# Transposed features made a stage ahead, two added steps, and small roots as powers on GpSimd

## The chip, the cores and the metric

The kernel runs on one core of a Trainium2 chip. A core has five engines that work through queues of their own, each strictly in its order: PE (TensorE, matrix products and transposes, with weight loads shown as PEld), DVE (VectorE, elementwise work and reductions), ACT (ScalarE, activation functions and copies), POOL (GpSimd) and SP (SyncE, which issues the DMAs here). Engines wait for one another through semaphores. The metric is the device time of one execution, in microseconds; the number shown for a kernel is the median of its runs.

## What is computed

The input is 64 independent graphs, each with 256 nodes of 128 features `x` and a 0/1 adjacency matrix `adj` (about 12% ones, symmetric, full diagonal). Four layers run one after the other; each adds its result to `x` and normalizes each node's features (mean 0, variance 1):

```python
# layer 0: for each node the maximum over its neighbours
pre = p[:, :, None, :] + q[:, None, :, :] + b        # p = x(W1-W2), q = x W2
h   = max(relu(pre) * adj[..., None], axis=2)
# layer 1: three ELU projections, two aggregations over adj, one product, tanh
# layer 2: ELU twice, then twice  D^-1/2 (adj+I) D^-1/2 (h W) + b,  D the degrees
# layer 3: for each pair of nodes a normalized message
pre = m_j[:, None, :, :] + m_i[:, :, None, :] + b1
msg = gelu(layernorm(pre, g1, be1))
agg = einsum('bijo,bij->bio', msg, adjacency)
out = layernorm(concat([x, agg]) @ W2 + b2, g2, be2)
```

Every normalization needs one over the square root of a variance, and layer 2 one over the square root of each node's degree.

## The kernel before

The features lie on the partitions or the nodes do, 128 at a time, so a graph has two halves (H = 2). The adjacency is sparse: a node's neighbours are numbered and nodes are sorted by their number of neighbours, so that one graph's pairs fit 4800 columns for each half (WIDTH), cut into five tiles of 1024 columns (the fifth has 704). `hot` is a one-hot matrix (fp8) that picks for each column its neighbour.

The work on one graph is split into four stages, written as generators: `first` (load `x` and `adj`, sort, build `hot`), `second` (`layer_0`, then `layer_1`), `third` (`layer_2`, then the first four tiles of layer 3) and `last` (the other six tiles, the messages, the output). In a steady step, `last` of graph g, `third` of g+1, `second` of g+2 and `first` of g+3 are interleaved by `together`: each generator runs up to its next `yield`, and the one that is relatively least far, by the number of its yields in `STAGES`, goes next. A scheduler of the framework then fixes each engine's order from that; it is the same in every steady graph. Where this text speaks of the built order, it means the order in which a built program holds the instructions of each engine.

The places that matter here (line numbers of the kernel before):

- `inverse_root` (L70 to L73): a square root on ACT (L72) and a reciprocal on DVE (L73). `layernorm` calls it on `rs`, 128x2, five times a graph (the variance is made ready at L172, the scale is used at L178, or at L182 and L183 for the output); `layer_2` on the degrees `dinv`, 128x2, once (L269 to L272); `sums_of` on `vr`, 128x16 or 108x16, five times, for pairs of tiles.
- [...]square root, gelu, exp and tanh need switches, which show as ACT_TABLE_LOAD on the line of the function that follows.
- `to_features` (L202 to L207): two transposes of a graph's features on PE (L205), and a copy of the result to SBUF on ACT (L207). `layer_0` begins with it for `xT_0`; the products with `w0qp` (L650) follow. Their result `q`, split into three bf16 parts (L497 to L500), is what the gathers of layer 0 (L668) read, and their maxima are folded on DVE (L492) into `lanes`.
- Layer 3's tiles: matmuls of L731 gather, DVE adds into `pre` (L735), ACT squares (L739), PE sums the squares over the features (L746), ACT makes a `row` (L748), which goes through DRAM (`line`) and comes back as `vr`, one column for each pair of nodes spread over partitions; its inverse root, times a mask (L772), goes through DRAM again (`scale_line`) and comes back broadcast as `rs_s`; DVE multiplies (L846), ACT applies the gelu (L848), DVE folds (`sums`, L492), PE multiplies with the weights (L867), ACT copies `ak` (L872), and PE brings it into the nodes' order (L877), for the output `y` (L328).

PE writes into PSUM banks of two pools, `mm` and `bigp`, four each.

Of the kernel before, what the change touches and what calls it, by code (L numbers as in the profile page):

```python
# [9 lines left out]
F32 = mybir.dt.float32  # L10
BF16 = mybir.dt.bfloat16
AF = mybir.ActivationFunctionType
ALU = mybir.AluOpType
# [6 lines left out]
P = 128  # L20
# [23 lines left out]
def kernel(  # L44
# [9 lines left out]
    nc = tc.nc  # L54
    B, N, D = x.shape
    assert N == 2 * P and D == P
    H = N // P
    Q = P // 4

    consts = ctx.enter_context(tc.tile_pool(name="consts", bufs=1))  # L60
# [6 lines left out]
    minus1 = consts.tile([P, 1], F32, name="minus1")  # L67
    nc.vector.memset(minus1, -1.0)

    def inverse_root(t):  # L70

        nc.scalar.activation(t, t, AF.Sqrt)  # L72
        nc.vector.reciprocal(t, t)  # L73

    def load(src, shape, name):
        t = consts.tile(shape, F32, name=name)
        nc.sync.dma_start(t, src)
        return t
# [4 lines left out]
    def spread(src, name):  # L83
        return load(bass.AP(tensor=src.tensor, offset=src.offset, ap=[[0, P], [1, P]]), [P, P], name)

    w0 = load(l0_w.rearrange("(c p) o -> p c o", p=P), [P, 2, P], "w0")
    w0qp = consts.tile([P, 2, P], F32, name="w0qp")
    nc.vector.tensor_copy(w0qp[:, 0], w0[:, 1])
    nc.vector.tensor_sub(w0qp[:, 1], w0[:, 0], w0[:, 1])
    b0 = column(l0_b, "b0")  # L90
    b0s = spread(l0_b, "b0s")

# [27 lines left out]
    with tc.tile_pool(name="prep", bufs=1) as prep, tc.tile_pool(  # L120
        name="ps_prep", bufs=2, space=bass.MemoryType.PSUM
    ) as ps_prep:

        def transposed(dst, src, shape, name, part=lambda t: t):
            t = prep.tile(shape, F32, name=name)
            nc.sync.dma_start(t, src)
            for d, s in part(t) if dst is None else [(dst, t)]:
                pt = ps_prep.tile([P, P], F32, name="pt")
                nc.tensor.transpose(pt, s, ident)
                nc.vector.tensor_copy(d, pt)  # L130

        transposed(w1_ioT[:, :P], l1_w_in, [P, P], "w1_in")
        transposed(w1_ioT[:, P:], l1_w_out, [P, P], "w1_out")
        transposed(w1_nodeT, l1_w_node, [P, P], "w1_node")
        transposed(
            None, l1_w_upd.rearrange("o (c k) -> o c k", k=P), [P, 3, P], "w1_upd",
            lambda t: [(w1_updT[:, c], t[:, c]) for c in range(3)],
        )
        w3 = prep.tile([P, 2, P], F32, name="w3")
        nc.sync.dma_start(w3, l3_w1.rearrange("(c p) o -> p c o", p=P))  # L140
        w3m = prep.tile([P, 2], F32, name="w3m")
        nc.vector.tensor_reduce(w3m, w3, AX.X, ALU.add)
        nc.vector.tensor_scalar(w3m, w3m, 1.0 / P, None, ALU.mult)
        for c in range(2):
            nc.vector.tensor_scalar(w3c[:, c], w3[:, c], w3m[:, c:c + 1], None, ALU.subtract)
        b3 = prep.tile([P, 1], F32, name="b3")
        nc.sync.dma_start(b3, bass.AP(tensor=l3_b1.tensor, offset=l3_b1.offset, ap=[[1, P], [1, 1]]))
        invp = prep.tile([P, P], F32, name="invp")
        nc.vector.memset(invp, 1.0 / P)
        pb = ps_prep.tile([P, P], F32, name="pt")  # L150
        nc.tensor.matmul(pb[:, :1], invp, b3, start=True, stop=True)
        nc.vector.tensor_sub(b3c, b3, pb[:, :1])


    class Shared:
# [5 lines left out]
        def psum(self):  # L161
            return self.ps_mm.tile([P, 512], F32, name="mm")
# [189 lines left out]
    def sparse(ctx):  # L352
# [36 lines left out]
        with tc.tile_pool(name="cs_prep", bufs=1) as pp:  # L389
            t = pp.tile([P, P], F32, name="upto_f")  # L390
# [4 lines left out]
            t = pp.tile([P, N], I32, name="iota_i")  # L395
# [3 lines left out]
            t = pp.tile([P, 1], I32, name="part_i")  # L399
# [25 lines left out]
            t = pp.tile([P, 1], F32, name="gbe")  # L425
# [9 lines left out]
            for i in range(3):  # L435
                t = pp.tile([3, P], BF16, name="u_part")
# [5 lines left out]
            t = pp.tile([ROWS, g_n, g_w], F32, name="tail_f")  # L442
# [12 lines left out]
        sh = Shared(work, state, ps_mm)  # L455
# [46 lines left out]
        def first(g, s):  # L502

            xn = state.tile([P, H, P], F32, name="x0", bufs=3)
# [25 lines left out]
            for hi in range(H):  # L530
                for h in range(H):
                    c = (hi * H + h) * 2
# [38 lines left out]
            permT = hold.tile([P, H, H, N], F32, name="permT")  # L571
# [17 lines left out]
            lack = hold.tile([ROWS, H, N], BF16, name="lack")  # L589
# [43 lines left out]
            for h in range(H):  # L633
# [5 lines left out]
                    saturate=False,  # L639
                )  # L640
            s["hot"] = hot

        def layer_0(s):

            xn, hot, lack, lack_t, permT = (s[n] for n in ("xn", "hot", "lack", "lack_t", "permT"))
            xT = sh.to_features(xn, "xT_0", 1)
            yield
            pq = psum()
            for h in range(H):
                nc.tensor.matmul(  # L650
                    pq[:, h * N:(h + 1) * N], xT[:, h * P:(h + 1) * P], w0qp.rearrange("p c o -> p (c o)"),
                    start=True, stop=True,
                )
            pq = pq.rearrange("p (h c o) -> p h c o", h=H, c=2)
            q3 = work.tile([P, 3, H, P], BF16, name="q3")
            split3(q3, pq[:, :, 0])
            own = work.tile([P, H, P], F32, name="own")
            for h in range(H):
                nc.vector.tensor_add(own[:, h], pq[:, h, 1], b0s)
            yield  # L660
            mk = work.tile([P, H, H, P], F32, name="mk")
            for h in range(H):
                lanes = work.tile([P, 2, N], F32, name="lanes")
                for t0 in range(0, WIDTH, 512):
                    tl = min(512, WIDTH - t0)
                    pt = ps_big.tile([P, 512], F32, name="bigp")
                    for i in range(3):
                        nc.tensor.matmul(  # L668
                            pt[:, :tl], q3[:, i, h], hot[:, h, t0:t0 + tl], start=i == 0, stop=False
                        )  # L670
                    todo = []
                    for s0, n, w, at in pieces(t0, t0 + tl):
                        if s0 >= g_s0:
                            todo.append((pt[:, at:at + n * w], low, lack_t[:, h].rearrange("p s k -> p (s k)")))
                            continue
                        for i in range(n):
                            m = SURE[s0 + i]
                            if m < w:
                                c = at + i * w
                                todo.append((pt[:, c + m:c + w], pick_of(s0 + i), lack[:, h, m:w]))  # L680
                    if not todo:
                        todo.append((pt[:, :2], pick_of(0), lack[:, h, 0:2]))
                    for i, (o_, l_, r_) in enumerate(todo):
                        nc.tensor.matmul(o_, l_, r_, start=False, stop=i == len(todo) - 1)  # L684
                    if t0 == 0:
                        nc.scalar.copy(lanes, pt.rearrange("p (s k) -> p s k", s=2))
                    else:
                        fold(lanes, pt, t0, tl, ALU.max)
                    yield
                mx = work.tile([P, N], F32, name="total_m")  # L690
                nc.vector.tensor_max(mx, lanes[:, 0], lanes[:, 1])
                pt = psum()
                for hk in range(H):
                    nc.tensor.transpose(pt[:, hk * P:(hk + 1) * P], mx[:, hk * P:(hk + 1) * P], ident)
                nc.scalar.copy(mk[:, h], by_half(pt))
                yield
            pm = psum()
            for h in range(H):
                for hi in range(H):
                    c = h * N + hi * P  # L700
                    for hk in range(H):
                        nc.tensor.matmul(
                            pm[:, c:c + P], permT[:, h, hk, hi * P:(hi + 1) * P], mk[:, h, hk],
                            start=hk == 0, stop=hk == H - 1,
                        )
            yield
            m0 = work.tile([P, H, P], F32, name="m0")
            nc.scalar.copy(m0, by_half(pm))
            nc.vector.tensor_max(m0, pm[:, N:].rearrange("p (h d) -> p h d", h=H), m0)
            nc.vector.tensor_add(m0, m0, own)  # L710
            y = work.tile([P, H, P], F32, name="y", bufs=2)
            nc.vector.scalar_tensor_tensor(y, m0, 0.0, xn, ALU.max, ALU.add)
            s["x1"] = sh.node_tile("x1")
            yield from sh.layernorm(s["x1"], y)
# [6 lines left out]
        def sums_of(s, i):  # L721
# [39 lines left out]
            n = at + tl  # L761
# [6 lines left out]
                fu[:rows],  # L768
                s["fulls"].rearrange("h w -> (h w)")[first_at:first_at + n].rearrange("(p k) -> p k", k=PIECE),
            )  # L770
            inverse_root(vr[:rows])
            nc.vector.tensor_mul(vr[:rows], vr[:rows], fu[:rows])  # L772
            out_line = dram.tile([1, GROUP * TILE], F32, name="scale_line")
            nc.sync.dma_start(out_line[:, :n].rearrange("o (p k) -> (o p) k", k=PIECE), vr[:rows])
# [108 lines left out]


        U = next(u for u in (UNROLL, 8, 4, 2, 1) if B % u == 0)
        STAGES = [(last, 34), (third, 34), (second, 42), (first, 17)]

        def steps(g0):
            ss = [{} for _ in range(U)]
# [262 lines left out]
```

## Time and profile before

| | |
|---|---|
| median of 3 runs | 5589.18 us (5588.3 to 5589.55) |
| the profiled execution | 5585.87 us, of which the span from first to last instruction is 5583.8 us |
| busy in the span | PE 4511.0, DVE 4805.5, ACT 4218.5, POOL 2.0 us |
| granted TensorE clock, mean | 0.876 of full speed |
| one graph in the steady stretch | about 85.3 us |
| ACT_TABLE_LOAD | 1152, 1283 ns each |

The page gives for each engine its busy time; groups of instructions by line have the mean time of one and what ended the idle time in front of them. "idle before" or "[4.30 <-ACT xT L207]" means that the engine stood still for 4.30 us in front of this instruction, and that the one named was the last that it waited for. In the chain that ended last, PE has 42%, DVE 34% and ACT 17% of the span.

### The profile page before, as it was taken

To read this page: it belongs to the slowest core of one execution; us is meant where nothing else is said; L and a number is where in the kernel's file an instruction comes from. 1 tells how busy PE (TensorE), PEld (TensorE's weight loads), DVE (VectorE), ACT (ScalarE), POOL (GpSimd) and SP (SyncE) were. 2 spreads that over 40 slices of the span, in tenths; PEclk is the share of its full clock that TensorE was granted. 3 is DMA by queue.
4 is the path that set the end of the run, shared out by engine and by line. 5 is a ranking of instruction groups with operands and counts; after the bars stand their busy time and mean duration, and the time that the engine had idled before them with its cause. 6 is when DMAs were issued, how large, how long until landed. Compare 5 with 4: busy or idle time off the path is not lost.

```text
span 5583.8 us, 83622 instructions
## 1 busy us (share of the span) xinstructions
PE 4511.0 (81%) x27408; PEld 2487.9 (45%) x27408; DVE 4805.5 (86%) x14654; ACT 4218.5 (76%) x6465; POOL 2.0 (0%) x10
## 2 busy tenths in 40 slices
PE   5888888888788888887887888888888878888884
PEld 3444444444444444444444444444444444444442
DVE  7788888898888888888988888889888888888886
ACT  2777777777777777777777777777777777777776
POOL 0000000000000000000000000000000000000000
PEclk8888888888888888888888888888888888888886
DMA  0212222222222122222222222221222222212212
GB/s 24 65 59 72 67 63 66 72 65 66 66 65 70 60 72 67 63 66 74 63 66 67 70 66 61 69 67 63 71 70 63 66 67 70 66 59 71 64 59 76
DMA packets 292814, 365.17 MB, mean 65 GB/s; under 512 B 151952, under 2 KB 210448, under 8 KB 292368
## 3 DMA queue, kind: packets, MB, share of 16 engines
q1 hardware_dynamic: 292368, 359.73, 20.8%
q8 instruction: 218, 3.57, 0.3%
q14 instruction: 228, 1.87, 0.1%
HBM read 345.07 MB, written 14.53 MB: 64 GB/s over the span
## 4 chain that ended last, share of the span: by engine, by line
PE 42%; DVE 34%; ACT 17%; issue 5%; DMA 3%; SPq 0%; DVEq 0%; POOL 0%; ACTq 0%; POOLq 0%
PE bigp L731 8%; PE bigp L668 8%; DVE lanes L492 8%; DVE pre L735 6%; ACT L72 6%; DVE hot L628 5%; DVE sums L492 5%; PE mm L867 4%; DVE pre L846 3%; PE mm L746 3%; PE mm L877 2%; PE mm L817 2%; PE mm L294 2%; DMA rs_s<-scale_line 2%; ACT sums L848 2%
## 5 line engine op out<-in xcount | busy, mean ns | idle before, releaser
L668 PE MATMUL bigp<-hot,q 128*128 128x512 fp8e4 (+1 forms) x3840 | 1117.5, 391 | 206.2 <-DVE lanes L492 179.7
L731 PE MATMUL bigp<-hot,c 128*128 128x512 fp8e4 (+1 forms) x3840 | 1010.6, 395 | 136.0 <-DVE pre L735 77.1
L735 DVE TENSOR_TENSOR pre<-bigp,dT 128x512 f32<-128x512 f32 (+6 forms) x1664 | 841.4, 534 | 252.2 <-PE bigp L731 245.9
L739 ACT ACTIVATE sq<-pre 128x1024 f32<-128x1024 f32 (+1 forms) x640 | 636.6, 995 | 273.2 <-DVE rs L73 196.9
L492 DVE TENSOR_TENSOR lanes<-bigp,lanes 128x512 f32<-128x512 f32 (+6 forms) x1536 | 769.3, 501 | 12.2 <-ACT vr L72 2.9
L846 DVE TENSOR_TENSOR pre<-pre,rs_s 128x1024 f32<-128x1024 f32 (+1 forms) x640 | 734.4, 1148 | 35.6 <-DMA rs_s<-scale_line 34.5
L492 DVE TENSOR_TENSOR sums<-pre,sums 128x1024 f32<-128x1024 f32 (+6 forms) x1024 | 628.3, 614 | 11.6 <-ACT pre L848 11.2
L848 ACT ACTIVATE pre<-pre,be,g 128x1024 f32<-128x1024 f32 (+1 forms) x512 | 600.0, 1172 | 11.0 <-DVE pre L846 6.9
L731 PEld LDWEIGHTS <-c 128*128 128x128 bf16 x3840 | 346.2, 102 | 544.5 <-issue 268.1
L848 ACT ACT_TABLE_LOAD x447 | 573.5, 1283 | 7.9
L72 ACT ACT_TABLE_LOAD x447 | 573.5, 1283 | 7.9
L748 ACT ACTIVATE row<-mm,eps_t 128x256 f32<-128x256 f32 (+1 forms) x640 | 293.5, 459 | 361.9 <-PE mm L746 351.0
L668 PEld LDWEIGHTS <-q 128*128 128x128 bf16 x3840 | 309.6, 100 | 514.9 <-DVE lanes L492 186.5
L746 PE MATMUL mm<-sq,ones 128*32 128x256 f32 (+1 forms) x5120 | 436.5, 418 | 113.7 <-ACT sq L739 110.7
L628 DVE TENSOR_SCALAR hot<-rank 128x512 fp8e4<-128x512 bf16 (+5 forms) x1536 | 485.4, 345 | 0.0
L684 PEld LDWEIGHTS <-pick 42*128 42x128 bf16 x2944 | 154.5, 95 | 449.6 <-issue 435.2
L650 PE MATMUL mm<-w0qp,xT 128*128 128x256 f32 x256 | 130.0, 662 | 266.3 <-ACT xT L207 266.3
L867 PE MATMUL mm<-w3u,sums 128*128 128x128 f32 x2048 | 293.8, 287 | 44.9 <-DVE sums L492 44.9
L867 PEld LDWEIGHTS mm<-w3u,sums 128*128 128x128 f32 x2048 | 258.7, 195 | 75.9 <-PE bigp L731 39.6
L684 PE MATMUL bigp<-lack,pick 42*128 42x36 bf16 (+16 forms) x2944 | 275.8, 187 | 0.0
L746 PEld LDWEIGHTS mm<-sq,ones 128*32 128x32 f32 x5120 | 107.2, 115 | 352.5 <-ACT sq L739 162.0
L73 DVE RECIPROCAL vr<-vr 128x16 f32<-128x16 f32 (+1 forms) x320 | 79.5, 249 | 161.7 <-ACT vr L72 161.6
(227 smaller groups left out, 7319.0 us busy)
## 6 DMA issues: line engine op xcount, KB each, us to landing
rs_s<-scale_line SPq DMA_DIRECT2D x512, 512.0 KB
rs_s<-scale_line SPq DMA_DIRECT2D x128, 352.0 KB
an<-in_adj SPq DMA_DIRECT2D x64, 256.0 KB
x<-in_x SPq DMA_DIRECT2D x64, 128.0 KB
line<-row SPq DMA_DIRECT2D x512, 4.0 KB
out<-o SPq DMA_DIRECT2D x64, 128.0 KB
fu<-fulls SPq DMA_DIRECT2D x192, 4.0 KB
vr<-line SPq DMA_DIRECT2D x192, 8.0 KB
```

What stands on the lines that cost most here:

```text
L72: nc.scalar.activation(t, t, AF.Sqrt)
L492: nc.vector.tensor_tensor(lanes[:, :k, :w], src[:, i:i + k], lanes[:, :k, :w], op)
L628: nc.vector.tensor_scalar(hot[:, :, at:at + w], rank[:, :, :w], s0 + i + 1.0 - FAR, None, ALU.is_equal, saturate=False)
L668: nc.tensor.matmul(pt[:, :tl], q3[:, i, h], hot[:, h, t0:t0 + tl], start=i == 0, stop=False)
L684: nc.tensor.matmul(o_, l_, r_, start=False, stop=i == len(todo) - 1)
L731: nc.tensor.matmul(pt[:, :bl], c3[:, k, h], hot[:, h, t0 + b:t0 + b + bl], start=k == 0, stop=k == 2)
L735: nc.vector.tensor_add(block(pre[:, b:], n, w, at), block(pt, n, w, at), widen(dT[:, h, :w], n))
L739: nc.scalar.activation(sq[:, :tl], pre[:, :tl], AF.Square)
L746: nc.tensor.matmul(pr[q * Q:(q + 1) * Q, :tl // 4], ones[:, :Q], v4[:, :, q], start=True, stop=True)
L846: nc.vector.tensor_mul(pre[:, :tl], pre[:, :tl], rs[:, :tl])
L848: nc.scalar.activation(msg[:, :tl], pre[:, :tl], AF.Gelu, bias=be3, scale=g3)
L867: nc.tensor.matmul(pt[:, cols], lanes[:, k, cols], w3u[:, 1], start=k == 0, stop=False)
```

## The change

- `inverse_root` becomes one operation on GpSimd: the tile to the power of a constant tile `mhalf` of -0.5. It serves the five norms and the degrees. The roots of `vr` keep ACT's square root and DVE's reciprocal, with a step boundary (`yield`) between the two.
- `xT_0` is made at the end of `first`, a stage earlier, in two buffers in place of one, and handed on in `s`; `layer_0` starts with the products.
- A step boundary is added in `layer_0` between the maximum of the two lanes and its transposes.
- The numbers of yields in `STAGES` follow. The load of `w0` and its two derived operations move among the preparations, into memory that is given back.

```diff
+    mhalf = consts.tile([P, H], F32, name="mhalf")
+    nc.vector.memset(mhalf, -0.5)
     def inverse_root(t):
-        nc.scalar.activation(t, t, AF.Sqrt)
-        nc.vector.reciprocal(t, t)
+        nc.gpsimd.tensor_tensor(t, t, mhalf[:t.shape[0], :t.free_size()], ALU.pow)
...
-    w0 = load(l0_w.rearrange("(c p) o -> p c o", p=P), [P, 2, P], "w0")
     w0qp = consts.tile([P, 2, P], F32, name="w0qp")
-    nc.vector.tensor_copy(w0qp[:, 0], w0[:, 1])
-    nc.vector.tensor_sub(w0qp[:, 1], w0[:, 0], w0[:, 1])
...
+        w0 = prep.tile([P, 2, P], F32, name="w0")
+        nc.sync.dma_start(w0, l0_w.rearrange("(c p) o -> p c o", p=P))
+        nc.vector.tensor_copy(w0qp[:, 0], w0[:, 1])
+        nc.vector.tensor_sub(w0qp[:, 1], w0[:, 0], w0[:, 1])
...
             s["hot"] = hot
+            s["xT"] = sh.to_features(xn, "xT_0")

         def layer_0(s):
-            xn, hot, lack, lack_t, permT = (s[n] for n in ("xn", "hot", "lack", "lack_t", "permT"))
-            xT = sh.to_features(xn, "xT_0", 1)
-            yield
+            xn, xT, hot, lack, lack_t, permT = (s[n] for n in ("xn", "xT", "hot", "lack", "lack_t", "permT"))
             pq = psum()
...
                 nc.vector.tensor_max(mx, lanes[:, 0], lanes[:, 1])
+                yield
                 pt = psum()
...
-            inverse_root(vr[:rows])
+            nc.scalar.activation(vr[:rows], vr[:rows], AF.Sqrt)
+            yield
+            nc.vector.reciprocal(vr[:rows], vr[:rows])
             nc.vector.tensor_mul(vr[:rows], vr[:rows], fu[:rows])
...
-        STAGES = [(last, 34), (third, 34), (second, 42), (first, 17)]
+        STAGES = [(last, 37), (third, 36), (second, 43), (first, 17)]
```

## The prediction

> **What bounds the kernel now.** I read the page first (parts 1 and 5), then, for ten whole graphs in the steady stretch (1096.1 to 1949.5 us), the busy time by engine, then who waited for whom on each engine, then the order in time around the longest wait.
>
> ```profile
> PE 4511.0 (81%) x27408; PEld 2487.9 (45%) x27408; DVE 4805.5 (86%) x14654; ACT 4218.5 (76%) x6465; POOL 2.0 (0%) x10
> ...
> 1096.10:1949.50 853.40, 701.53 (x4282) 386.48 (x4282) 745.55 (x2272) 658.76 (x1011) 0.00 (x0) 0.88 0.21 67
> ```
>
> The second line is the stretch of ten graphs (PE, PEld, DVE, ACT, POOL busy us, granted clock, DMA share, GB/s). A graph takes 85.3 us; DVE works 74.6 us of them and stands still for 10.8. No other engine is as full, DVE works in order, and so a graph's time is DVE's work plus DVE's waits. The waits of the ten graphs, DVE first and then PE:
>
> ```profile
> DVE pre L735 <- PE bigp L731: 39.4, 50, 2.0
> DVE vr L73 <- ACT vr L72: 24.1, 20, 2.2
> DVE io L224 <- PE mm L221: 11.8, 10, 1.2
> DVE y L254 <- ACT y L252: 9.0, 10, 0.9
> DVE y L328 <- PE mm L877: 8.3, 10, 0.8
> ...
> PE mm L650 <- ACT xT L207: 43.0, 10, 4.3
> ```
>
> Columns: us in total, times, longest. Per graph: 3.9 us for the matmuls of `pre`, 2.4 for ACT's root of `vr`, 1.2 for `io`, 0.9 for the tanh, 0.8 for the output. PE's largest wait is 4.3 us, for one copy. In time (PE, then ACT, then DVE, of one graph):
>
> ```profile
> 1101.66 0.39 PE L516 MATMUL mm<-ident_b,nz 128*128 128x128 bf16 x4
> 1106.35 2.08 PE L650 MATMUL mm<-w0qp,xT 128*128 128x256 f32 x4 [4.30 <-ACT xT L207]
> ...
> 1102.01 1.28 ACT L252 ACT_TABLE_LOAD   x1
> 1103.31 0.42 ACT L252 ACTIVATE y<-y 128x256 f32<-128x256 f32 x1
> 1103.74 1.28 ACT L72 ACT_TABLE_LOAD   x1
> 1105.03 0.32 ACT L72 ACTIVATE rs<-rs 128x2 f32<-128x2 f32 x2
> 1105.26 0.77 ACT L739 ACTIVATE sq<-pre 128x704 f32<-128x704 f32 x1
> 1105.94 0.35 ACT L207 COPY xT<-mm 128x256 f32<-128x256 f32 x1
> ...
> 1113.70 0.69 DVE L735 TENSOR_TENSOR pre<-bigp,dT 128x512 f32<-128x512 f32 x1 [1.02 <-PE bigp L731]
> 1116.48 0.69 DVE L735 TENSOR_TENSOR pre<-bigp,dT 128x512 f32<-128x512 f32 x1 [1.95 <-PE bigp L731]
> ```
>
> The transpose is done at 1101.8, but its copy stands on ACT behind two table loads, the tanh, two roots and a square. PE is 4.3 us late, and seven microseconds later DVE pays 1.0 and 1.9 us. A faster PE alone moves the graph too: the only two short graphs (84.0 and 83.4 us, near 2550 us) are those with a granted clock of 0.90 and 0.92 in place of 0.88.
>
> [...]The trace has 1283 ns on each of 1152 loads[...] (the load at 1102.01 is followed by its tanh 1.30 us later); I use 1.28. [...]
>
> **The change, part by part.** Per graph, against 85.3 us.
>
> (1) Six roots (five `rs`, one `dinv`) leave ACT and DVE. ACT loses 384 activations of 0.2 us (59.3 + 13.0 = 72 us), and the built order of the changed kernel holds 1016 table loads where before has 1152: 136 x 1.283 = 174 us. ACT falls from 4218 to about 3972 us busy. It isn't the bound, so that is worth only what it shortens of waits. DVE loses 384 reciprocals; they last 0.159 us, but the next instruction starts 0.08 us after one: 0.08 x 6 = 0.5 us gained a graph, directly.
>
> (2) `xT_0` a stage earlier. In the built order the two transposes still stand right in front of L650 on PE, but their ACT copy now comes after `ag` and one `row`, ahead of the tanh's load. PE's wait becomes transpose end to copy to matmul, 0.35 us of copy plus two handovers, say 0.7 in place of 4.3. What PE did meanwhile (L516) comes after L650. What is late next: the second wait of L735 stays in part, because the first fold on DVE (L492) now waits for ACT's copy of `lanes`, which stands behind a gelu, a load and the `vr` root. Of 2.9 us I keep 1.2: 1.7 gained. The tanh moves behind the `xT_0` copy, but DVE now has two z steps, an L846 (1.14) and L331 between L251 and L254, about 2.5 us, so its 0.9 us wait goes: 0.9 gained. No DMA is added; the second buffer of `xT_0` is memory only.
>
> (3) The added steps. Between ACT's root of `vr` and its reciprocal another step's DVE work is now queued (an L735 in two of five places, a fold or a hot step in the rest). Of 2.4 us I keep 0.8, since ACT is a solid chain of loads and gelus there: 1.6 gained. Nothing stands behind it at DVE but what stood there before; the DMAs from `vr` (SP, L774, then `rs_s`) are due later by one DVE instruction, 0.6 us, against 0.55 us a graph of DMA wait now.
>
> (4) A new queueing on ACT: at the end of a graph the root of `vr` with its load (1.28 + 0.2) now stands ahead of the copy `ak`, where before `ak` came first. `ak` feeds L877, on which L328 waits already (0.8). PE also runs L746, L236 and L238 first. L328 is later by some 1.5 us, of which 0.6 is covered by the dinv work put ahead of it: 0.9 lost.
>
> (5) The powers. Behind each on POOL stands only the next power. On DVE the readers wait: `x1` (L178) has just one 0.3 us hot step between its variance and its scale, dinv the 0.4 us L509, z and o some 0.8, x2 0.6, x3 1.7. [...]part of the dinv wait hides in L328's: 1.6 us in all. With D the length of one power and 0.1 us for its handovers, the cost is 6 x (D + 0.1) - 1.6 = 6D - 1.0 us. D isn't in the trace. Nearest rows: the iota of one element on POOL, 224 ns, is the floor; the whole root on the old route, 1.28 + 0.20 + 0.16 = 1.64 us, is the top I allow. I take D = 0.5, twice the fixed part: 2.0 us lost (floor 0.3, top 8.8).
>
> (6) Start-up: the load of `w0` moves on SP from first place to behind twenty-three other loads and its two DVE copies with it. PE first waits 15.0 us for `w_in`, and `w0qp` is first read at 47.8 us: nothing, and at most one DMA issue, 0.5 us, without that cover. The `mhalf` memset is one small DVE instruction.
>
> Sum: gained 0.5 + 1.7 + 0.9 + 1.6 = 4.7; lost 0.9 + 2.0 = 2.9; net 1.8 us of 85.3. Over 64 graphs 115 us. The profiled execution's span was 5583.8 us, its own time 5585.9, the median of the runs 5589.2; a change of 115 us against the one is the same against the other: **5474 us**.
>
> **Rivals.**
>
> *The power is slow.* Without POOL the net gain is 4.7 - 0.9 = 3.8 us, so the sign turns where 6D - 1.0 = 3.8, at D = 0.8 us, at the reader of `rs`, `x1` most of all. With D = 1.2: 6.2 - 3.8 = 2.4 us lost, 154 us in all: 5743. For it: an operation with no row[...]; six of them in series with the engine that bounds. Against: two elements per partition only. Chance 0.23.
>
> *DVE's waits nearly all go.* With D at its floor (0.3), no loss in (4), and all of 2.9, 2.4 and 0.9 gained: 0.5 + 2.9 + 2.4 + 0.9 - 0.3 = 6.4 us, 410 us: 5180; half of the extra over my forecast gives about 5330, which I take for this case. For it: ACT has 250 us less, and most waits named above end at ACT. Against: the fresh order has chains of its own (L302 now stands behind seven matmuls of L668, and L306 on DVE waits for it). Chance 0.14.
>
> *The new order stalls elsewhere.* L306 comes up on DVE right after one L846 while L302 is still behind on PE; 3 us there would turn the net to -1.2: 5666. The power is then as cheap as I say. Chance 0.07.
>
> *Nothing moves.* The gains in (2) and (3) only reappear as the wait for the next PE result: about 5589. Chance 0.06. That the change doesn't do what it says I exclude: the built order has the powers on POOL and the copy in its new place.
>
> **The numbers.** My forecast has 0.50, the four rivals 0.23, 0.14, 0.07 and 0.06. Within 0.2% (11 us) is what a measurement of this kernel can tell from no change. Faster 0.50 + 0.14 = 0.64, same 0.06, slower 0.30. The likeliest case alone spans 5400 to 5550 (the gains of (2) and (3) one microsecond up or down). For 8 in 10 the range runs from 5260, near the second rival, to 5745, the first with D = 1.2; D at 1.64 (8.8 - 3.8 = 5 us, 5909) stays outside.
>
> **What would show it.** Right: a graph of about 83.5 us; PE's wait before L650 under 1 us; ACT near 3970 us with 1016 loads; L252's wait on DVE gone; `vr` waits near 1 us a graph; DVE waits on POOL of about 2 us a graph, the `x1` reader first. Wrong: powers over 0.8 us each; DVE instructions on SBUF that lengthen while POOL works; L306 or L328 waiting over 2 us; a granted clock below 0.87.

## The result, and the profile after

The changed kernel takes 5538.0 us (median of 4 runs, 5534.4 to 5545.2) where the kernel before takes 5589.4 (5588.3 to 5590.1): a ratio of 0.991, with a 95% interval of 0.9898 to 0.9922. That is 51 us gained, where the forecast had 115. The profiled execution has a span of 5539.2 us.

Line numbers have moved by 2 to 5: L650 is now L652, L735 is L738, L328 is L331, L275 is L278, L306 is L309, L746 is L749, L867 is L872. The root of `vr` and its reciprocal are L774 and L776, and the power is L75. First the busy line of the page and the stretch of ten graphs (PE, PEld, DVE, ACT, POOL busy us, granted clock, DMA share, GB/s):

```profile
PE 4460.2 (81%) x27408; PEld 2478.9 (45%) x27408; DVE 4759.2 (86%) x14271; ACT 3993.4 (72%) x5945; POOL 282.7 (5%) x394
...
1086.50:1933.25 846.75, 694.24 (x4281) 387.03 (x4281) 738.42 (x2212) 625.03 (x930) 43.90 (x60) 0.92 0.22 67
```

ScalarE is 225 us less busy and DVE 46, close to what the forecast's step (1) had (3972 against 3993 us on ScalarE). A graph now takes 84.7 us in this stretch; DVE works 73.8 of them and stands still for 10.8, as long as before. So in DVE's account the whole gain is its lighter work, and its waits were not shortened in sum, they were exchanged. DVE's waits of the ten graphs (us in total, times, longest):

```profile
DVE y L331 <- PE mm L882: 21.7, 10, 2.6
DVE hs L309 <- PE mm L305: 18.0, 20, 2.3
DVE aT L278 <- PE mm L239: 12.6, 8, 2.1
DVE vr L776 <- ACT vr L774: 11.4, 20, 1.0
DVE x L181 <- POOL rs L75: 6.6, 10, 0.7
DVE dinv L275 <- POOL dinv L75: 5.8, 10, 0.6
...
DVE lanes L495 <- ACT lanes L688: 4.9, 10, 0.5
DVE lanes L495 <- PE bigp L686: 4.1, 6, 1.1
...
DVE o L181 <- POOL rs L75: 3.4, 10, 0.3
DVE z L186 <- POOL rs L75: 3.2, 10, 0.3
```

Gone are the 3.9 us a graph for `pre`, the 1.2 for `io` and the 0.9 for the tanh; `vr` is down from 2.4 to 1.1. In their place stand the output's add (0.8 before, 2.2 now), `hs` (1.8) and `aT` (1.3), both of layer 2, the fold of the `lanes` (0.9) and four readers of a power (1.9). PE, in the same stretch:

```profile
PE mm L749 <- ACT sq L742: 65.0, 32, 3.3
...
PE mm L652 <- ACT xT L210: 4.9, 10, 0.5
```

and the first of these lines as it was before:

```profile
PE mm L746 <- ACT sq L739: 14.6, 10, 1.5
```

The 4.3 us wait that the change aimed at is 0.5. But PE now waits 6.5 us a graph for `sq` at the matmul of L749, where it waited 1.5 before. And the powers themselves (mean ns of one after the comma):

```profile
L75 POOL TENSOR_TENSOR rs<-rs,mhalf 128x2 f32<-128x2 f32 x320 | 230.4, 727 | 4386.0 <-DVE rs L175 4052.5 <-DVE mv L173 226.7 <-DVE lanes L495 75.5
L75 POOL TENSOR_TENSOR dinv<-dinv,mhalf 128x2 f32<-128x2 f32 x64 | 50.4, 787 | 843.5 <-DVE dinv L272 843.5
```

That waits were exchanged for waits doesn't say yet what sets the length of a graph. Two things in the trace do not fit a plain sum of DVE's waits. Of 53 graphs of the steady stretch, 50 were 85.2 to 85.8 us long before, most of them 85.3; after, in one and the same order of instructions, they last 81.2 to 88.8 us, 12 of them under 82 and 30 over 85. And the granted clock rose from 0.876 to 0.914. Its records hold only two values, full and half, in stretches that are whole multiples of 3.413 us: 1392 us at half clock before, 959 after, or 3.0 and 2.3 stretches a graph. Cut along these edges, the graph that the prediction showed in order of time looks like this (window, length, then PE, PEld, DVE, ACT, POOL busy us, granted clock, DMA share, GB/s):

```profile
1098.27:1101.69 3.42, 3.31 (x33) 2.03 (x32) 3.33 (x22) 2.27 (x5) 0.00 (x0) 1.00 0.36 81
1101.69:1105.10 3.41, 0.35 (x6) 0.18 (x3) 2.41 (x12) 3.35 (x5) 0.00 (x0) 1.00 0.63 227
1105.10:1108.51 3.41, 2.16 (x8) 1.33 (x12) 3.26 (x9) 3.38 (x8) 0.00 (x0) 0.51 0.37 119
1108.51:1111.93 3.42, 3.15 (x16) 1.05 (x13) 1.20 (x6) 3.37 (x7) 0.00 (x0) 0.50 0.01 3
1111.93:1115.34 3.41, 3.41 (x13) 1.07 (x11) 1.58 (x7) 2.61 (x3) 0.00 (x0) 0.50 0.46 109
1115.34:1118.75 3.41, 3.41 (x22) 1.69 (x21) 2.27 (x6) 2.29 (x6) 0.00 (x0) 0.99 0.61 210
```

PE works 0.35 us in the second window, because of the 4.3 us wait; the next three windows are granted half the clock, until one of them is full of work (3.15 us was not enough), and DVE, busy 3.3 us a window before, falls to 1.2 and 1.6. At half the clock the matmuls ran at half the speed: in a run of those of 512 columns (L668, L731) one starts 426 ns after the other there, and 216 ns at full clock, in the median. The changed kernel does the same at another place:

```profile
1373.49:1376.90 3.41, 1.25 (x11) 0.50 (x15) 3.05 (x14) 3.40 (x5) 0.00 (x0) 1.00 0.58 192
1376.90:1380.31 3.41, 3.41 (x15) 1.63 (x7) 3.25 (x8) 3.38 (x6) 0.00 (x0) 0.50 0.20 74
1380.31:1383.73 3.42, 3.42 (x21) 1.76 (x20) 1.25 (x4) 0.57 (x2) 0.00 (x0) 1.00 0.04 4
```

Behind the first 200 us of the trace before, the clock fell to half only behind windows in which PE was busy 0 to 55% of the time, and rose again only behind windows at 84% or more; the trace after gives 60% and 86%. Not every such window brought it back: the one of 3.15 us above is at 92%, so the busy share is not all that counts. It fell behind the first window of the changed kernel above, which had one wait of 2.2 us, and in the trace before behind one with two of 0.8 and 1.1 us (313 us into it).

### The profile page after: what moved, and what is told of

It is laid out like the page before. It is cut to its first block, busy times and chain, and to the rows that moved or that the text cites. A ratio compares the mean times of both kernels' runs of the same rounds, so it can differ in the third digit from the quotient of the medians.

```text
span 5539.2 us, 83909 instructions
## 1 busy us (share of the span) xinstructions
PE 4460.2 (81%) x27408; PEld 2478.9 (45%) x27408; DVE 4759.2 (86%) x14271; ACT 3993.4 (72%) x5945; POOL 282.7 (5%) x394
## 5 line engine op out<-in xcount | busy, mean ns | idle before, releaser
L670 PE MATMUL bigp<-hot,q 128*128 128x512 fp8e4 (+1 forms) x3840 | 1086.3, 377 | 66.9 <-DVE pre L738 60.6
L734 PE MATMUL bigp<-hot,c 128*128 128x512 fp8e4 (+1 forms) x3840 | 950.8, 369 | 159.3 <-DVE pre L738 126.1
L738 DVE TENSOR_TENSOR pre<-bigp,dT 128x512 f32<-128x512 f32 (+6 forms) x1664 | 859.5, 537 | 7.0 <-PE bigp L734 6.6
L749 PE MATMUL mm<-sq,ones 128*32 128x256 f32 (+1 forms) x5120 | 468.3, 419 | 421.0 <-ACT sq L742 414.9
L631 DVE TENSOR_SCALAR hot<-rank 128x512 fp8e4<-128x512 bf16 (+5 forms) x1536 | 501.0, 355 | 0.0
L75 POOL TENSOR_TENSOR rs<-rs,mhalf 128x2 f32<-128x2 f32 x320 | 230.4, 727 | 4386.0 <-DVE rs L175 4052.5
L872 PE MATMUL mm<-w3u,sums 128*128 128x128 f32 x2048 | 370.8, 333 | 90.6 <-ACT elu_e L195 74.9
L749 PEld LDWEIGHTS mm<-sq,ones 128*32 128x32 f32 x5120 | 113.6, 113 | 611.5 <-ACT sq L742 501.6
L872 PEld LDWEIGHTS mm<-w3u,sums 128*128 128x128 f32 x2048 | 323.8, 237 | 122.1 <-ACT elu_e L195 87.4
L208 PE MATMUL mm<-ident,x 128*128 128x128 f32 x512 | 151.3, 318 | 215.1 <-DVE x L181 215.0
```

Source lines behind the costliest of these rows:

```text
L631: nc.vector.tensor_scalar(hot[:, :, at:at + w], rank[:, :, :w], s0 + i + 1.0 - FAR, None, ALU.is_equal, saturate=False)
L670: nc.tensor.matmul(pt[:, :tl], q3[:, i, h], hot[:, h, t0:t0 + tl], start=i == 0, stop=False)
L734: nc.tensor.matmul(pt[:, :bl], c3[:, k, h], hot[:, h, t0 + b:t0 + b + bl], start=k == 0, stop=k == 2)
L738: nc.vector.tensor_add(block(pre[:, b:], n, w, at), block(pt, n, w, at), widen(dT[:, h, :w], n))
L749: nc.tensor.matmul(pr[q * Q:(q + 1) * Q, :tl // 4], ones[:, :Q], v4[:, :, q], start=True, stop=True)
L872: nc.tensor.matmul(pt[:, cols], lanes[:, k, cols], w3u[:, 1], start=k == 0, stop=False)
```

## The experiments

Three questions: which part of the change moved the time, what the half-clock stretches cost, and what the powers cost. Any edit gives the whole kernel a new order, since its scheduler orders all instructions afresh. Where an experiment kept the order, this is said; there the comparison is of one thing.

### The parts alone

`e1_xt`: only the transposed features, on the kernel before (with the load of `w0` in the preparation, as in the diff).

```
+            s["xT"] = sh.to_features(xn, "xT_0")        # end of first
-            xT = sh.to_features(xn, "xT_0", 1)          # layer_0
-            yield
-        STAGES = [..., (second, 42), ...]
+        STAGES = [..., (second, 41), ...]
```

> The kernel before with one part of the change: the transposed features made a stage earlier (and the load of w0 moved, which makes room for their second buffer). Theory A (TensorE's clock: the 4.3 us wait before L650 is followed by a stretch at half clock, and the L735 waits of 3.9 us a graph come from that): PE's wait goes below 1 us, the half-clock stretch at 10 us into the graph goes, the L735 waits fall below 1 us, and the time falls by 2 to 4 us a graph, to 5330 to 5460 us. Theory B (what pays is the relief of ScalarE by the powers): the PE wait goes, but the waits only move, 5570 to 5600 us. Theory C (each edit is a new order of the whole kernel, with stalls of its own, and the parts do not add up): anywhere between 5450 and 5700, with new DVE waits that neither kernel has.

Measured: 5648.5 us, ratio 1.0105 (1.0088 to 1.0122): slower. PE's longest waits in ten graphs:

```profile
PE mm L746 <- ACT sq L739: 70.4, 20, 5.5
PE mm L650 <- ACT xT L208: 37.3, 10, 3.7
```

Theory A falls at its first step. The features are in `first`, yet the wait before L650 is still 3.7 us a graph, since in this order their copy stands as late on ScalarE as ever; and a 5.5 us wait for `sq` is new.

`e2_pow`: only the powers for `rs` and `dinv`; `vr` keeps its root with the reciprocal right behind it.

```
-        nc.scalar.activation(t, t, AF.Sqrt)
-        nc.vector.reciprocal(t, t)
+        nc.gpsimd.tensor_tensor(t, t, mhalf[:t.shape[0], :t.free_size()], ALU.pow)
```

> The kernel before with one part of the change: the roots of the norms and the degrees as powers on GpSimd (the root of vr stays on ScalarE with its reciprocal right behind it). Theory A: the readers of the powers wait 1.5 to 2.5 us a graph on POOL, the roots taken from DVE give back 0.7, and the 4.3 us wait of PE before the xT_0 copy shrinks by the table load that left (1.3 us) but does not go: 5620 to 5680 us. Theory B: ScalarE is 200 us less busy and the waits that end at it shrink by more than the powers cost: 5500 to 5550 us. Theory C: between 5450 and 5700, with DVE waits that neither kernel has.

Measured: 5577.9 us, ratio 0.9984 (0.9977 to 0.9991), outside the ranges of theories A and B. The readers of powers wait 3.3 us a graph, more than expected, and still the graph is 85.3 us long, as before; PE's wait before L650 is 2.6. A cost of some three microseconds, and gains of as much elsewhere, left the graph at the same length.

`e3_steps`: only the two added steps.

```
+                yield                          # after the maximum of the lanes
+            yield                              # between vr's root and its reciprocal
-        STAGES = [(last, 34), (third, 34), (second, 42), (first, 17)]
+        STAGES = [(last, 37), (third, 36), (second, 44), (first, 17)]
```

> The kernel before with one part of the change: the two added steps (after the root of vr and after the maximum of the lanes) and the step counts that go with them. Theory A: the vr waits fall from 2.6 to about 1.2 us a graph, the 4.3 us wait of PE and the L735 waits stay, the output's add waits up to 1 us longer: 5540 to 5600 us. Theory B: 5570 to 5600 us, since ScalarE has the same work. Theory C: between 5450 and 5700, the vr waits shorter and others longer.

Measured: 5932.2 us, ratio 1.062 (1.0602 to 1.0637), with 1880 us at half clock, outside the range of every theory. The steps that were to shorten the `vr` waits left 3.0 us a graph on one of them.

`e4_nopow`: the changed kernel with the roots back on ScalarE and DVE (the opposite of the diff of `e2_pow`).

> The changed kernel with one part undone: the roots of the norms and the degrees are again a square root on ScalarE and a reciprocal on DVE. Theory A: the 1.9 us a graph of waits on POOL go, 0.7 us of root work comes back, PE's wait before the layer-0 matmuls stays below 1 us: 5440 to 5500 us. Theory B: ScalarE has 200 us more work and the gain is lost: 5580 to 5620 us. Theory C: between 5450 and 5700, and the difference to the changed kernel is not the opposite of what the powers alone did to the kernel before.

Measured: 5590.6 us, ratio 1.0007 (0.9999 to 1.0016) to the kernel before: the whole gain is gone. The time lies in theory B's range and in C's.

So the parts don't add. Alone they give +1.05%, -0.16% and +6.2%; together -0.9%. This is what theory C says, though `e3_steps` went beyond its range, and it warns against such a list of parts itself: each row is one draw of the order. Which part "brought" the 51 us has no answer here.

### What half clock costs

In these kernels, which are taken from the kernel before or the changed one, PE repeats a matmul or a transpose in front of one of its waits. The result is written again and nothing comes earlier. The places were chosen so that ScalarE and DVE keep the order of the kernel compared with.

`f1_fill`, on the kernel before:

```
-            for h in range(H):
-                nc.tensor.transpose(pt[:, h * P:(h + 1) * P], xn[:, h], ident)
+            for h in range(H * {'xT_0': 8}.get(name, 1)):
+                nc.tensor.transpose(pt[:, h % H * P:(h % H + 1) * P], xn[:, h % H], ident)
```

> The kernel before, with one thing added and the order of every engine as it was: the two transposes in front of the 4.3 us wait of PE are made eight times instead of once (the same result written again), so that PE works some 3 us of the 4.3 us it stood still. Nothing is moved and nothing comes earlier. Theory D (the L735 waits come from TensorE's clock, which falls to half after a window of 3.4 us with too little work): the half-clock stretch about 10 us into each graph goes, the L735 waits of 2.9 us a graph at that place fall below 1 us, the granted clock rises from 0.876 to above 0.91, and the time falls by 1 to 3.4 us a graph, to 5370 to 5525 us. Rival E (the waits come from PE being late by 4.3 us with its queue behind it, whatever its clock): more work on PE can't help, 5580 to 5620 us, and the L735 waits stay at 2.9 us.

Measured: 5584.4 us, ratio 0.9992 (0.9983 to 1.0001). The repeated transposes were shorter than I had reckoned, 0.11 us each, and PE still waits 2.8 of the 4.3 us. The stretch at 10 us stayed in 33 of the 53 graphs and came one or two windows later in the others. This is inconclusive, but for one thing: with 142 us less at half clock the graph is again 85.3 us in the mean.

`f5_fill20` is the same with `'xT_0': 20`.

> The kernel before with the transposes in front of the 4.3 us wait made twenty times (eight times covered only 1.5 us of it: a repeated transpose takes 0.11 us), all orders as before. Theory D: PE's wait before L650 falls to 0 to 0.5 us, the half-clock stretch that began 10 us into each graph goes, and of the L735 waits of 2.9 us at most 1.2 are left; the time is 5430 to 5560 us, or stays at 85.3 us a graph only if another stretch takes its place. Rival E: the L735 waits stay at 2.9 us.

Measured: 5494.9 us, ratio 0.9827 (0.981 to 0.9843). With more work on PE and nothing earlier, 94 us are gained, so rival E cannot be the whole. The wait before L650 is gone and no stretch begins at 10 us, but in 37 of 53 graphs one begins at 14 or 17 us. Of the two `pre` waits there, 2.9 us before, 2.2 are left, where theory D had at most 1.2: in this order PE now waits 2.0 us, where it waited 0.3, for the next copy on ScalarE (L668 for `q`). So a quarter of the `pre` waits went when PE was kept busy. The rest belongs to the late chain of copy, matmul and copy, as E has it, or to the stretch that now begins later; this run does not part them.

`f2_fill3` fills three places: `'xT_0': 8, 'xT_1': 3`, and eight times

```
+                    for _ in range({(1, 4096): 8}.get((h, t0), 0)):
+                        nc.tensor.matmul(pt[:, :tl], q3[:, 0, h], hot[:, h, t0:t0 + tl], start=True, stop=True)
```

> The kernel before with work repeated on PE at three places in front of its waits (the transposes before the 4.3 us wait, a bigp matmul before the 2.9 us wait for the lanes, the transposes of x1 before the 1.1 us wait for pre), the order of DVE and ScalarE as before. Theory D: two or all three half-clock stretches of a graph go, the granted clock is above 0.93 and the time is at or below that with one place filled, 5250 to 5480 us. Rival E: 5580 to 5700 us, since PE has some 5 us more work a graph.

Measured: 5430.4 us, ratio 0.9728 (0.9701 to 0.9755). Half clock is down to 757 us, 2.0 stretches a graph, and many graphs last 81.8 to 81.9 us.

`f3_fillafter`, on the changed kernel, fills two places:

```
+                    for _ in range({(1, 1536): 6}.get((h, t0), 0)):
+                        nc.tensor.matmul(pt[:, :tl], q3[:, 0, h], hot[:, h, t0:t0 + tl], start=True, stop=True)
+                for _ in range({(4, 0): 5}.get((i, b), 0)):
+                    nc.tensor.matmul(pt[:, :bl], c3[:, 0, h], hot[:, h, t0 + b:t0 + b + bl], start=True, stop=True)
```

> The changed kernel with work repeated on PE at two places where its half-clock stretches begin (six bigp matmuls before the L749 wait 40 us into the graph, five before the L734 wait 80 us into it), the order of DVE and ScalarE as in the changed kernel. Theory D: the stretches behind those two places go, the long graphs (85.6 us) turn into short ones (81.2 us), the waits for aT and y at the graph's end fall by 1 to 2 us, granted clock above 0.93: 5300 to 5450 us. Rival E: 5530 to 5600 us.

Measured: 5392.3 us, ratio to the kernel before 0.9651 (0.9635 to 0.9667). It beats both kernels, with eleven matmuls more per graph. The stretch 40 us into the graph is gone, the one at 80 us is left in 20 of 53 graphs, and the waits for `aT` and `hs` fell from 1.3 and 1.8 to 0.4 and 1.3 us a graph.

`f4_placebo` repeats as many matmuls where PE is busy anyway: `{(1, 3072): 6}` and `{(2, 0): 5}` in the same two loops.

> The changed kernel with the same eleven bigp matmuls repeated as in the run that filled two waits, but in stretches where PE is busy anyway (six about 45 us into the graph, five about 62 us into it), the orders of DVE and ScalarE practically those of the changed kernel. Theory D (only windows in which PE has too little work matter): no gain, the half-clock stretches stay where they were, 5530 to 5600 us. Rival F (any shift of PE against the other engines or any extra PE work would have done it): 5390 to 5480 us.

Measured: 5545.5 us, ratio 0.9916 (0.9899 to 0.9932), the changed kernel's own 0.991. Rival F falls: it isn't the extra work or the shift, it is where the work stands.

`f6_fillmore` adds to `f3_fillafter` five matmuls 50 us into the graph:

```
+            if i == 9:
+                pw = psum()
+                for _ in range(5):
+                    nc.tensor.matmul(pw, c3[:, 0, h], hot[:, h, t0:t0 + 512], start=True, stop=True)
```

> The changed kernel with its two filled places and five more repeated bigp matmuls ahead of the transposes of x3, 50 us into the graph, where the last regular half-clock stretch begins; orders of DVE and ScalarE as in the changed kernel. Theory D: the stretch there shrinks from two windows to one or none, 5300 to 5385 us. Rival: the 3.3 us wait behind those transposes stays empty and only moves the stretch by a window, 5385 to 5420 us.

Measured: 5391.8 us, ratio 0.9648 (0.9632 to 0.9664): half clock fell further, from 661 to 547 us, and the time did not. The time lies in the rival's range. What became shorter is the stretch that begins 50 us into the graph (6.8 to 5.5 us a graph), and in `f4_placebo` the same stretch was shortened too (6.4 to 4.7) without a gain. So this stretch doesn't set the time, and what bounds these graphs is something else.

### What the powers cost

`e5_pow2`: a second power ahead of each, into a spare tile; PE's order as in the changed kernel, DVE's and ScalarE's nearly.

```
+        nc.gpsimd.tensor_tensor(spare, t, m, ALU.pow)
         nc.gpsimd.tensor_tensor(t, t, m, ALU.pow)
```

> The changed kernel with a second power on GpSimd ahead of each of the six (on the same input, into a spare tile that nobody reads), the order of PE as it was and those of DVE and ScalarE nearly so. If each power's length is paid in full by DVE, as the prediction's step (5) has it beyond its cover: 6 x 0.69 = 4.1 us a graph, 5740 to 5830 us. If the time beside the powers is filled and only the reader right behind waits: about half of it, 5620 to 5720 us. If the graph's length is set by windows of the clock rather than by the sum of DVE's work and waits: it snaps to 85.3 or 88.7 us a graph, 5590 to 5610 or about 5800 us.

Measured: 6077.8 us, ratio 1.089 (1.0871 to 1.0908), 540 us more than the changed kernel and beyond every expectation. DVE's waits in ten graphs:

```profile
DVE lanes L499 <- PE bigp L690: 35.6, 45, 1.6
...
DVE x L185 <- POOL rs L79: 24.1, 30, 1.4
...
DVE o L185 <- POOL rs L79: 10.4, 10, 1.0
```

The waits for POOL are 4.7 us a graph, 2.8 more than before the doubling: if waits added, that would make about 180 us. The largest wait is for PE, which was at half clock for 1915 us, twice as long as in the changed kernel. DVE's own work did not lengthen beside the powers (739.4 us in ten graphs, 738.4 in the changed kernel). What lengthens is the power: with nothing of DVE beside it, it takes 0.69 us, and 1.19 us behind DVE's product with `rs_s` (L855, 128x704), which takes 0.885 us there and 0.887 elsewhere.

`e6_mult`: the same instruction with a product in place of the power; all engines in exactly the order of the changed kernel.

```
-        nc.gpsimd.tensor_tensor(t, t, mhalf[:t.shape[0], :t.free_size()], ALU.pow)
+        nc.gpsimd.tensor_tensor(t, t, mhalf[:t.shape[0], :t.free_size()], ALU.mult)
```

> The changed kernel with the power replaced by a product with a constant in the same instruction on GpSimd (the roots are left out, so the values differ), every instruction of every engine in the same place. It measures what a power costs beyond the simplest operation on that engine, and what a shorter one would be worth. If the product takes 0.2 to 0.3 us where the power takes 0.69: the waits for POOL fall from 1.9 to about 0.2 us a graph. If these add to the rest one for one: 5420 to 5450 us. If the clock's windows decide: more than that, 5300 to 5420 us, with fewer half-clock stretches, or no change at all. If the product takes as long as the power, the time is that of the changed kernel.

Measured: 5591.2 us, ratio 1.0005 (0.9996 to 1.0014). The product takes 0.23 us where the power takes 0.73, the waits for POOL shrink from 1.9 to 0.2 us a graph, and the kernel is 53 us slower than with the power, which no expectation had. Half clock is up from 959 to 1090 us, and the stretch 40 us into the graph begins in 40 of 53 graphs instead of 32.

`g7_mult_fill` is `e6_mult` with the three places of `f6_fillmore` filled, in exactly that kernel's order.

> The changed kernel with its three filled places and, in it, the power replaced by a product with a constant (the roots are left out, so the values differ), every instruction in the same place as in the kernel with the three filled places. If what failed in the forecast's sum is that the clock answers to each shift, then with the clock held up the waits add again: the 1.9 us a graph for POOL go and the time falls by 60 to 130 us, from 5392 to 5260 to 5330 us, with at most 1.5 half-clock stretches a graph. If DVE's waits don't add for some other reason (they move to the next result from PE or ScalarE): 5370 to 5410 us, with the waits for y and aT longer by what POOL's lose.

Measured: 5394.1 us, ratio 0.9648 (0.9632 to 0.9664): the same as with the power. First the waits of ten graphs in `f6_fillmore`:

```profile
DVE y L331 <- PE mm L890: 20.3, 10, 3.0
DVE vr L784 <- ACT vr L782: 10.6, 19, 1.0
...
DVE x L181 <- POOL rs L75: 6.6, 10, 0.7
DVE dinv L275 <- POOL dinv L75: 5.8, 10, 0.6
```

and then in `g7_mult_fill`:

```profile
DVE y L331 <- PE mm L890: 23.2, 10, 2.7
DVE vr L784 <- ACT vr L782: 19.5, 20, 2.0
...
DVE pre L859 <- DMA rs_s<-scale_line: 8.9, 13, 1.3
...
DVE x L181 <- POOL rs L75: 1.6, 10, 0.2
```

What POOL's waits lose (19.0 to 1.6 us in ten graphs), `vr` (+8.9), the broadcast scales (3.3 before, +5.6), `aT` (4.0 to 7.2) and `y` (+2.9) take back. This is the second expectation, though `vr` and the broadcast scales take more than `y` and `aT`. So the clock is not the whole reason: even with it held up (612 us at half clock, 547 with the power), DVE's waits do not add. DVE comes earlier to results that ScalarE, PE and the DMA queue deliver no earlier.

`g8_pow2_fill` is `e5_pow2` with the same three places filled (DVE's and ScalarE's order again nearly that of `f6_fillmore`).

> The changed kernel with its three filled places and a second power ahead of each of the six, into a spare tile that nobody reads. Doubling the powers cost the changed kernel 540 us, of which the longer waits for POOL explain 2.6 us a graph, 166 us. If the clock made the rest: 5530 to 5620 us here, and fewer than 3 half-clock stretches a graph. If doubled powers cost 540 us by other means[...]: 5850 to 5950 us.

Measured: 5795.5 us, ratio 1.037 (1.0353 to 1.0388), 404 us over `f6_fillmore`. Neither expectation held: the clock was not held up. PE's waits for the normed features are longer (6.0 us a graph at L212, 2.8 at L208 in `f6_fillmore`) and open a new low window, and a stretch begins 14 us into all 53 graphs examined (1206 us at half clock in all). DVE's work is 737.4 us in ten graphs, 737.1 in `f6_fillmore`, so DVE's instructions take no longer in sum, and other means than the clock were not shown. Of the 404 us, POOL's waits would make 180, if waits added; that the rest is the clock agrees with the trace (DVE waits 3.6 us a graph for `lanes` right behind that stretch), but is not shown apart.

The two families in which the order was kept (nearly, in the two with doubled powers), in one table (half clock: us of the profiled execution):

| kernel | time | half clock |
|---|---|---|
| before | 5588 | 1392 |
| `f1_fill` | 5584 | 1250 |
| `f5_fill20` | 5495 | 826 |
| `f2_fill3` | 5430 | 757 |
| changed | 5538 | 959 |
| `e5_pow2` | 6078 | 1915 |
| `e6_mult` | 5591 | 1090 |
| `f4_placebo` | 5545 | 874 |
| `f3_fillafter` | 5392 | 661 |
| `f6_fillmore` | 5392 | 547 |
| `g7_mult_fill` | 5394 | 612 |
| `g8_pow2_fill` | 5796 | 1206 |

The trend is plain, the scatter too: the placebo has 85 us less at half clock than the changed kernel and no gain. It matters where in the graph a stretch lies.

## Why the prediction was right or wrong

The direction and the range held; the size did not: 0.7 us a graph in the ten graphs (51 us over 64, or 0.8) in place of 1.8. Step by step:

**(1) The roots off ScalarE and DVE.** Right: ScalarE 3993 us busy, forecast 3972; DVE's work fell by 0.7 us a graph, forecast 0.5.

**(2) The features a stage earlier.** PE's wait is 0.5 us, forecast 0.7; the tanh wait went, as forecast. But I kept 1.2 of the `pre` waits, and all 3.9 went, with 1.1 of `io` besides. `f5_fill20` shows one cause that the step lacked: with PE kept busy and nothing earlier, a quarter of the two large ones goes.

**(3) The added steps.** Right in this order: 1.3 to 1.4 us gained on `vr`, forecast 1.6. `e3_steps` shows that the same steps in another order leave a 3.0 us wait there.

**(4) The root of `vr` ahead of `ak`.** Right place, too small: the output's add lost 1.3 us, not 0.9, and `aT` 1.3 in the same spot; at 2.2 us it passed the 2 us that I had named as a sign of being wrong. In the long graphs PE is at half clock here; with two of the low windows filled, `aT` waits 0.4.

**(5) The powers.** The waits are what the step said, 1.9 us against 2.0, the reader of `x1` first, but that is luck: a power takes 0.73 us and not 0.5, for which the step's own 6D - 1.0 gives 3.4 us, and a larger cover than I had counted made up for it. The 1.6 us of cover and the 0.1 us of handovers in that formula were estimates of mine, and not shown; so was D = 0.5, about twice the 224 ns of one iota. DVE paid nothing in its own work where it met a power: in `e5_pow2` it is the power that lengthens (1.19 us behind L855, 0.69 alone), not DVE's L855 (0.885 us there, 0.887 elsewhere). As a cost the step is wrong: `e6_mult` takes 1.7 of the 1.9 us away and gains nothing, with the low windows filled (`g7_mult_fill`) or not. The break-even of the slow-power rival at D = 0.8 rested on the same addition. Towards longer powers the addition fails the other way: the doubling costs three times its waits.

**The rivals.** "The new order stalls elsewhere" named L306 (now L309) behind a late L302; it does wait 1.8 us a graph, not the 3 of the rival. "Nothing moves", with its waits that reappear at the next result, was given 0.06, and describes DVE's standing still (10.8 us before and after) better than my forecast did.

**The step that failed** is the sum itself: "a graph's time is DVE's work plus DVE's waits", with each wait priced alone. As an account it holds after the fact; as a forecast it does not. The sum had 4.2 us a graph of waits gained and 2.9 lost; in the ten graphs 7.7 were gained and 7.8 lost. Of the lost ones `hs` (1.8, named in a rival alone), `aT` (1.3), the fold of `lanes` (0.9) and the ELU steps (0.5) had no term. The experiments show two ways in which such a sum fails. A wait that was shortened returned at the next results of other engines: 1.7 us a graph taken away, and 5394 us against 5392 (`g7_mult_fill`). And PE's own waits, which the sum gave no price, decided on PE's clock in the next windows: eleven repeated matmuls a graph bring 146 us in front of two of them and nothing elsewhere (`f3_fillafter` against `f4_placebo`). The forecast noted that the only short graphs had a higher clock, and drew no price from it. How much of the missing 64 us is owed to each of the two is not shown.

Open is what bounds the graph at 81 to 82 us once the clock is held up (0.96 in the ten graphs of `f6_fillmore`), and which part of the change the new order owes its gain to.

## What to carry to other kernels

Where matmuls come in bursts, read the granted clock window by window before adding up waits: here a wait on PE had a second price, paid by the matmuls behind it (one every 426 ns in place of 216), and eleven repeated matmuls a graph in front of two such waits were cheaper than the waits, by 146 us. The waits that an edit takes from the busiest engine, or adds to it, are no forecast of what it brings, in either direction: here 1.7 us a graph taken away brought nothing, and 2.8 us added cost 8.4. And where a scheduler orders everything afresh, a part tried alone measures a new order, so keep the order fixed, or don't read the difference as the part's worth.

## What the runs showed of the hardware

- The clock granted to PE, behind the first 200 us of the 16 traces and in the windows of 3.413 us of their records, fell behind windows in which PE was busy 0 to 66% of the time, and always behind those under 42%; it rose only behind windows of 80% and more. That was not enough by itself: 357 of 2514 windows at half clock in which PE was busy throughout did not bring it back. What else counts is open. (In the start-up of the two kernels with doubled powers it also fell behind one window at 88 and one at 90%.)
- In some of these kernels the mean graph is a whole number of these windows. The kernel before, `e2_pow` and `f1_fill` differ in their waits, and all have graphs of 85.3 us in the mean, 25 windows; in `g8_pow2_fill` they are 88.7, 26 windows. In `e2_pow` single graphs last 84.8 to 85.9 us, yet over 53 of them the start of L652 stays within 0.5 us of one place in the window. A mean of 85.3 us alone doesn't prove it: the graphs of `e6_mult` have it too, but last 82.3 to 88.1 us and have no such place. That the edges of the windows make the graphs settle, so that small gains and losses don't show, is argued from these times and not shown by an experiment.
- A power of 128x2 elements on GpSimd took 0.69 us in the changed kernel with nothing of DVE beside it, and 0.73 in the mean of the `rs` (0.79 for `dinv`, which runs beside L512). Behind L855 in the doubled kernel (`e5_pow2`) it took 1.19 us in the median, and DVE's instruction was not lengthened (0.885 us there, 0.887 elsewhere). The same instruction with a product took 0.23 us (0.30 for `dinv`) in `e6_mult`.
